# Loading weight blocks from two hardware queues in the first stage of a cross-attention kernel

## The chip, the cores and the metric

The kernel runs on one core of one Trainium2 chip. Its time is device microseconds from start to end of one execution; several executions are made and their median is given. A profile is one further execution, recorded by the hardware profiler, with a time of its own. Inside it, times are counted in microseconds (us) from the start of its span. The engines are TensorE (PE in the profile; its weight loads are PEld), VectorE (DVE), ScalarE (ACT), GpSimd (POOL) and SyncE (SP). SP does no arithmetic: it issues loads and stores. ScalarE computes, and it can issue loads from a queue of its own too. A load moves data from the chip's main memory (HBM) to the on-chip memory of 128 partitions.

## The reference

The kernel computes multi-head cross-attention with a residual and a layer norm. `x` is 16 batches of 256 rows of 256 numbers; the context `c` is 16 batches of 77 rows of 192. There are 8 heads of width 256.

```python
Q = (x @ Wq).reshape(16, 256, 8, 256).transpose(0, 2, 1, 3)
K = (c @ Wk).reshape(16, 77, 8, 256).transpose(0, 2, 1, 3)
V = (c @ Wv).reshape(16, 77, 8, 256).transpose(0, 2, 1, 3)
score = einsum('bhqd,bhkd->bhqk', Q, K) / sqrt(256)
score = where(mask, score, -inf)
attn = softmax(score, axis=-1)
out = einsum('bhqk,bhkd->bqhd', attn, V).reshape(16, 256, 2048) @ Wo + x
out = (out - mean(out)) * rsqrt(var(out) + 1e-5) * gamma + beta
```

All data is float32. Wq is 256 x 2048, Wk and Wv are 192 x 2048, Wo is 2048 x 256.

## The kernel before

**What is folded.** Per head, scores need x Wq Wk^T c^T. The kernel first forms G = Wk Wq^T per head (tiles `gA` for the first 128 context features, `gB` for the other 64), then a = G^T c^T per batch and head (`pa` in PSUM, `a` in the on-chip memory), and then scores = x a. In the same way it forms Wv Wo per head (`pu`, `pw`; `uA`, `uB`). So there is a first stage of some 53 us that works on weights, and then a loop over 16 batches which works on x.

**The first stage.** Heads are taken in four pairs, a = 0 to 3. For pair 0, Wk and Wq are loaded as natural rows (`wk_nat`, two loads of `wq_nat`, two of `wk_last`), and TensorE transposes them: `turn_k` (L666), `turn_q(0)` and `turn_q(1)` (L658) and `turn_k_last` (L672). ScalarE and VectorE copy the results from PSUM: L667 (ScalarE, kT), and for each `turn_q` one copy on VectorE and one on ScalarE (both L661). `g_of(e)` multiplies the two (L753) and ScalarE scales the result into `gA` (L756). `turn_c` turns the first context rows, loaded as `c_sb` (L690; copies L121 and L123). `rest_of_g` makes `gB` (L763, L770). `a_of_pairs` makes `a` for the first four batches (L173 and L185 on TensorE, copies L811 on ScalarE).

For pairs 1 to 3, Wk and Wq are loaded as blocks: the 128 partitions are taken as four groups of 32, and each group is one load of one pair's Wk (96 KB, tile `wk_blk`) or Wq (128 KB, tile `wq_blk`), in rows of 512 bytes. `load_blocks` issues the four loads of one pair and matrix (L576). VectorE transposes the 32 x 32 blocks (`turn_blk`, L679, two instructions a pair: Wk, then Wq), and `g_of_pair` (L777, scaled by ScalarE at L785) and `rest_of_g_of_pair` (L793, scaled by VectorE at L802) follow.

**The order of work.** It is written out by hand: each engine executes its instructions in the order of the program, and only waits for data or buffers. At the end of the stage's front part the calls are

```python
turn_k()
turn_q(0)
g_of(0)
turn_q(1)
turn_k_last()
g_of(1)
turn_c()
rest_of_g()
turn_blk(1)
a_of_pairs(0)
for a in range(1, NF):
    g_of_pair(a)
    if a == 2:
        turn_blk(3)
    rest_of_g_of_pair(a)
```

with `turn_blk(2)` and `a_of_pairs(1)` at the end of the round a = 1. All loads stand ahead of this, on SP's queue, in this order: `wk_nat`, two of `wq_nat`, two of `wk_last`, `c_sb`, then for each pair 1 to 3 four of `wk_blk` and four of `wq_blk`, then 16 of `wvT`, four of `wo` (the last two go into the place of `wq_blk` and wait until that has been read), six for the rest of the context (`load_rest`), the mask (`bias`) and two sets of transposed x (`load_xT`). ScalarE issues no load; its first instruction is the load of its function table (L609). TensorE starts with 12 transposes of an identity matrix, whose result is not used (`keep_busy`, L640).

Each load tells of its landing on one of eight semaphores, which are given to the loads in turn.

Of the kernel before, what the change touches and what calls it, by code (L numbers as in the profile page):

```python
# [17 lines left out]
D = 256  # L18
EPS = 1e-05
GB = 4  # L20
# [5 lines left out]
def kernel(  # L26
# [13 lines left out]
    nc = tc.nc  # L40
    B, S, DI = x.shape
# [6 lines left out]
    GT = GB * QT  # L48
    NF = H // 2
    KR = S2 - KM  # L50
    BK = 32
    NM = P // BK
# [53 lines left out]
    def flat(ap):  # L106
        return ap.rearrange("p a b -> p (a b)")

    def half(i):
        return slice(i * LB, (i + 1) * LB)  # L110
# [7 lines left out]
    def evacuate(dst, src):  # L118
        evacs[0] += 1
        if evacs[0] % 2:  # L120
            nc.scalar.copy(dst, src)  # L121
        else:
            nc.vector.tensor_copy(dst, src)  # L123
# [5 lines left out]
    def in_two(name, shape, g):  # L129
        return pools[g % 2].tile(shape, F32, tag=f"{name}{g % 2}", name=f"{name}_{g}", bufs=1)  # L130

    def load_xT(g, lo=0, hi=GT):


        if lo == 0:
            xT_of[g] = in_two("xT", [P, GT * NM, 2, BK], g)
        rows = x.rearrange("b s d -> (b s) d")[(g * GT + lo) * P : (g * GT + hi) * P, :]
        rows = rows.rearrange("(m r) (i n) -> i r m n", r=BK, i=NM)
        for i in range(NM):
            nc.sync.dma_start(  # L140
                xT_of[g][i * BK : (i + 1) * BK, lo * NM : hi * NM].rearrange(
                    "p m n q -> p m (n q)"
                ),
                rows[i],
            )
# [412 lines left out]
    with tc.tile_pool(name="wonce", bufs=1) as wp:  # L558
# [4 lines left out]
        wq_nat = wp.tile([P, 2, 2 * D], F32, tag="wq", name="wq_nat")  # L563
# [3 lines left out]
        wq_blk = wp.tile([P, NF - 1, DI // BK, P], F32, tag="wqb", name="wq_blk")  # L567
        wk_blk = wp.tile([P, NF - 1, NL, P], F32, tag="wkb", name="wk_blk")
        wq_blocks = wq.rearrange("(m r) (a i f) -> a i r m f", r=BK, a=NF, i=NM)
        wk_blocks = wk.rearrange("(m r) (a i f) -> a i r m f", r=BK, a=NF, i=NM)  # L570
        wq_rows = wq[:, : 2 * D].rearrange("(t p) f -> p t f", p=P)
        wk_ends = wk[P:, : 2 * D].rearrange("r (e f) -> r e f", e=2)

        def load_blocks(to, blocks):
            for i in range(NM):
                nc.sync.dma_start(to[i * BK : (i + 1) * BK], blocks[i])  # L576


        rest = slice(first * CR, None)
# [2 lines left out]
        def load_rest():  # L582

            blocks = c.rearrange("b k l -> (b k) l")[rest].rearrange("(m r) l -> r m l", r=BK)
            for l in range(NL):
                i, of = (l, cA) if l < NM else (l - NM + LB // BK, cB)
                nc.sync.dma_start(
                    flat(of)[i * BK : (i + 1) * BK, rest].rearrange("p (m q) -> p m q", q=BK),
                    blocks[:, :, l * BK : (l + 1) * BK],
                )  # L590
# [7 lines left out]

        nc.sync.dma_start(wk_nat, wk[:P, : 2 * D])
        for e in range(2):  # L600
            nc.sync.dma_start(wq_nat[:, :, e * D : (e + 1) * D], wq_rows[:, :, e * D : (e + 1) * D])
        for e in range(2):
            nc.sync.dma_start(wk_last[half(e)], wk_ends[:, e])
        nc.sync.dma_start(c_sb, c_rows[:, :first, :])
        for a in range(1, NF):
            load_blocks(wk_blk[:, a - 1], wk_blocks[a])
            load_blocks(wq_blk[:, a - 1], wq_blocks[a])

        nc.scalar.preload_act_table_set("natural_log_exp_and_others")  # L609

        wvT = wp.tile([P, NF, NL, P], F32, tag="wvT", name="wvT")
        wo_of = [
            wp.tile([P, 2, 4, DI], F32, tag=tag, name=f"wo_{i}") for i, tag in enumerate(("wo", "wqb"))
        ]
        wv_blocks = wv.rearrange("(m r) (a i f) -> a i r m f", r=BK, a=NF, i=NM)
        wo_rows = wo.rearrange("(a p n) f -> a p n f", p=P, n=4)
        for a in range(NF):
            load_blocks(wvT[:, a], wv_blocks[a])
        for a in range(NF):
            nc.sync.dma_start(wo_of[a // 2][:, a % 2], wo_rows[a])  # L620
        load_rest()
        mask_row = mask.rearrange("b k -> (b k)")

        def load_bias(lo, hi):
            nc.sync.dma_start(
                bias_f[:, lo * S2 : hi * S2].bitcast(I32),
                mask_row[lo * S2 : hi * S2].partition_broadcast(P),
            )

        load_bias(0, GB)  # L630
        load_xT(0, 0, GT // 2)
        load_xT(0, GT // 2, GT)
        load_bias(GB, B)


        idle = ps_mm.tile([P, P], F32, tag="mm", name="idle")

# [16 lines left out]
        def turn_q(e):  # L654
            for dc, copy in enumerate((nc.vector.tensor_copy, nc.scalar.copy)):
                pt = ps_mm.tile([P, 2, P], F32, tag="mm", name=f"pt_q_{e}_{dc}")
                for t in range(2):
                    nc.tensor.transpose(  # L658
                        pt[:, t], wq_nat[:, t, e * D + dc * P : e * D + (dc + 1) * P], ident
                    )  # L660
                copy(qT[:, e, dc], flat(pt))  # L661

        def turn_k():
            pt = ps_mm.tile([P, 4, P], F32, tag="mm", name="pt_k")
            for n in range(4):
                nc.tensor.transpose(pt[:, n], wk_nat[:, n * P : (n + 1) * P], ident)  # L666
            nc.scalar.copy(kT_03[:, 0, :, :P], pt)  # L667
# [9 lines left out]
        def turn_blk(a):  # L677
            for blk, of in ((wk_blk, kT_blk), (wq_blk, qT_blk)):
                nc.vector.transpose(  # L679
                    of[a].rearrange("p n (m r) -> p m n r", r=BK),  # L680
                    blk[:, a - 1].rearrange("p m (n c) -> p m n c", c=BK),
                )

        def turn_c():
            for r in range(0, first, 2):
                n = min(2, first - r)
                pc = ps_mm.tile([P, 4, P], F32, tag="mm", name=f"pc_{r}")
                for lc in range(2):
                    for j in range(n):
                        nc.tensor.transpose(  # L690
                            pc[:, 2 * lc + j, :CR],
                            c_sb[:, r + j, lc * LB : lc * LB + P],
                            ident[:CR, :CR],
                        )
                rows = slice(r * CR, (r + n) * CR)
                evacuate(flat(cA)[:, rows].rearrange("p (j m) -> p j m", m=CR), pc[:, :n, :CR])
                evacuate(
                    flat(cB)[LB:, rows].rearrange("p (j m) -> p j m", m=CR),
                    pc[LB:, 2 : 2 + n, :CR],
                )  # L700
                nc.gpsimd.tensor_copy(flat(cB)[:LB, rows], flat(cB)[LB:, rows])
# [47 lines left out]
        def g_of(e):  # L749

            pg = ps_mm.tile([P, DI], F32, tag="mm", name=f"pg_{e}")
            for dc in range(2):
                nc.tensor.matmul(  # L753
                    pg, kT[:, e, dc, :P], qT[:, e, dc], start=(dc == 0), stop=(dc == 1)
                )
            nc.scalar.mul(gA[:, e], pg, D ** -0.5)  # L756

        def rest_of_g():

            ph = ps_mm.tile([P, DI], F32, tag="mm", name="ph")  # L760
            for dc in range(2):
                for e in range(2):
                    nc.tensor.matmul(  # L763
                        ph[half(e)],
                        kT[:, e, dc, P:],
                        qT[:, e, dc],
                        start=(dc == 0),
                        stop=(dc == 1),
                    )
            nc.vector.tensor_scalar(gB[:, 0], ph, D ** -0.5, None, ALU.mult)  # L770

        def g_of_pair(a):

            banks = [ps_mm.tile([P, DI], F32, tag="mm", name=f"pgb_{a}_{e}") for e in range(2)]
            for n in range(4):
                for e in range(2):
                    nc.tensor.matmul(  # L777
                        banks[e],
                        kT_blk[a][half(e), n, :P],
                        qT_blk[a][half(e), n],  # L780
                        start=(n == 0),
                        stop=(n == 3),
                    )
            for e, o in enumerate(banks):
                nc.scalar.mul(gA[:, 2 * a + e], o, D ** -0.5)  # L785
# [26 lines left out]

        turn_k()
        turn_q(0)
        g_of(0)
        turn_q(1)
        turn_k_last()
        g_of(1)
        turn_c()
        rest_of_g()  # L820
        turn_blk(1)
        a_of_pairs(0)
        for a in range(1, NF):
            g_of_pair(a)
            if a == 2:
                turn_blk(3)
            rest_of_g_of_pair(a)
            if a == 1:
                turn_blk(2)
                a_of_pairs(1)  # L830
# [190 lines left out]
```

## Time and profile before

| | |
|---|---|
| Median of 3 runs | 274.46 us (274.32 to 274.80) |
| The profiled execution's own time | 274.61 us |
| Its span (first to last instruction) | 272.8 us |
| Around the span | 1.8 us |
| TensorE busy, share of the span | 265.8 us, 97% |
| VectorE | 214.1 us, 78% |
| GpSimd | 170.4 us, 62% |
| ScalarE | 136.2 us, 50% |
| Loads and stores | all on one hardware queue, 21.77 MB |
| Loads of `wk_blk` | 12 of 96 KB, median 4.6 us from issue to landing |
| Loads of `wq_blk` | 12 of 128 KB, median 4.7 us |
| Loads of `wvT` | 16 of 96 KB, median 3.6 us |

A line of the timeline gives start and duration in us, the engine, the line of the kernel, the operation, output <- input with their shapes, the number of instructions merged, and in brackets how long the engine had been idle before and what ended that. A line of the chain that ended last gives start, duration and what. A line of the waits gives who waited for whom, the total in us, how many times, and the longest. A line of a table by stretches gives the stretch, its length, the busy time of PE, PEld, DVE, ACT and POOL (with numbers of instructions), the TensorE clock granted, the share of time that the 16 DMA engines were busy, and GB/s. PE's busy time is modelled: the matmuls are pipelined, so that a group's duration can reach past the start of the next.

### The profile page before, as it was taken

Reading aid. Unit: us, or ns where it says so; the run is one execution under the profiler, and the core shown is the slowest. Engines: PE = TensorE matmul, PEld = TensorE weight load, DVE = VectorE, ACT = ScalarE, POOL = GpSimd, SP = SyncE. Lnnn points to the kernel's source line nnn. Section 1 sums busy time; section 2 is a strip of 40 time slices with the busy share of each in tenths; the row PEclk is TensorE's granted clock in tenths of the full one; section 3 lists DMA queues with packets and bytes.
Section 4 is the critical chain, followed back from the end, with each engine's and each line's share of the span. In section 5 each row is a group of like instructions: output and inputs, shape, how many; then the busy total and the mean of one; then the engine's idle time right before and its main releaser. Section 6 shows DMA issues by size and latency. Waiting matters only on the chain.

```text
span 272.8 us, 14124 instructions
## 1 busy us (share of the span) xinstructions
PE 265.8 (97%) x6312; PEld 194.3 (71%) x6312; DVE 214.1 (78%) x418; ACT 136.2 (50%) x444; POOL 170.4 (62%) x231
## 2 busy tenths in 40 slices
PE   7999999999999999999999999999999999999992
PEld 6557486867494949495959586867796969694662
DVE  0554938589759898979799897878798989889875
ACT  3233225363918182827364646464546372927652
POOL 1000002809887878687878777777788789845754
PEclk9999999999999999999999999999999999999999
DMA  6999989940000322310221405000504061010102
GB/s 191 194 198 189 305 160 183 278 53 2 2 5 4 88 35 73 124 44 4 70 52 36 87 19 180 31 16 9 116 2 120 2 197 41 5 43 4 61 22 77
DMA packets 42460, 22.66 MB, mean 83 GB/s; under 512 B 23632, under 2 KB 41632, under 8 KB 42400
## 3 DMA queue, kind: packets, MB, share of 16 engines
q1 hardware_dynamic: 42400, 21.77, 34.8%
q8 instruction: 49, 0.80, 1.3%
q14 instruction: 11, 0.09, 0.1%
HBM read 17.57 MB, written 4.19 MB: 80 GB/s over the span
## 4 chain that ended last, share of the span: by engine, by line
PE 89%; DMA 7%; DVE 1%; SPq 1%; issue 0%; DVEq 0%
PE ps L283 25%; PE pa L173 11%; PE po L416 10%; PE pv L208 10%; PE pm L416 9%; PE pv L219 6%; PE pa L185 5%; DMA wq_blk<-in_L_xattn_Wq_dram 5%; PE po L348 4%; PE pu L717 3%; PE pr L242 2%; DMA c_sb<-in_ctx_dram 2%; PE pw L731 1%; PE pr L254 1%; PE po L364 1%; PE pgb L777 1%
## 5 line engine op out<-in xcount | busy, mean ns | idle before, releaser
L312 ACT ACTIVATE e<-s,top 128x77 f32<-128x77 f32 x256 | 66.8, 346 | 73.4 <-DVE top L305 73.4
L283 PE MATMUL ps<-a,xT 128*32 128x154 f32 x2048 | 70.0, 294 | 0.0
L326 POOL TENSOR_TENSOR p<-e,rden 128x512 f32<-128x512 f32 x64 | 47.8, 768 | 31.8 <-DVE rden L320 16.6
L283 PEld LDWEIGHTS ps<-a,xT 128*32 128x32 f32 x2048 | 66.0, 110 | 1.5 <-issue 0.8
L298 DVE TENSOR_TENSOR s<-ps,bias 128x308 f32<-128x308 f32 x64 | 29.7, 473 | 14.7 <-PE ps L283 14.6
L449 POOL TENSOR_TENSOR xg<-xg,m 128x256 f32<-128x256 f32 x39 | 28.6, 733 | 12.8 <-DVE xg L463 10.7
L173 PE MATMUL pa<-cA,gA 128*32 128x308 f32 (+1 forms) x576 | 36.4, 394 | 0.0
L173 PEld LDWEIGHTS pa<-cA,gA 128*32 128x32 f32 x576 | 18.4, 110 | 20.3 <-issue 9.1
L208 PE MATMUL pv<-uA,cA 128*32 128x512 f32 x256 | 30.4, 592 | 0.0
L318 DVE TENSOR_REDUCE den<-e 128x8 f32<-128x616 f32 x32 | 24.9, 777 | 5.1 <-ACT e L312 4.9
L305 DVE TENSOR_REDUCE top<-s 128x8 f32<-128x616 f32 x32 | 25.4, 795 | 1.1
L336 DVE STREAM_TRANSPOSE pT<-p 128x640 f32<-128x640 f32 x32 | 25.1, 813 | 0.9 <-POOL p L326 0.9
L379 POOL TENSOR_TENSOR ts<-vw 128x768 f32<-128x768 f32 x13 | 23.9, 1839 | 0.0
L532 DVE SCALAR_TENSOR_TENSOR xg<-xg,rstd,bet 128x256 f32<-128x256 f32 x26 | 20.9, 803 | 1.9
L185 PE MATMUL pa<-cB,gB 64*32 64x308 f32 (+1 forms) x576 | 20.3, 392 | 0.0
L922 ACT COPY vw<-pv 128x512 f32<-128x512 f32 x32 | 17.1, 584 | 6.3 <-PE pv L219 6.3
L185 PEld LDWEIGHTS pa<-cB,gB 64*32 64x32 f32 x576 | 10.7, 107 | 12.3 <-issue 9.2
L594 POOL COPY cRA<-cA 128x208 f32<-128x208 f32 x1 | 0.4, 358 | 29.8 <-DVE cA L593 29.8
L416 PE MATMUL po<-vr,pT 128*32 128x128 f32 x416 | 18.5, 273 | 0.0
L922 ACT COPY a<-pa 128x308 f32<-128x308 f32 (+1 forms) x56 | 17.5, 416 | 0.0
L219 PE MATMUL pv<-uB,cB 64*32 64x512 f32 x256 | 17.4, 601 | 0.0
L463 DVE TENSOR_TENSOR xg<-po,xg 128x256 f32<-128x256 f32 x31 | 11.7, 415 | 5.0 <-PE po L416 4.6
(117 smaller groups left out, 408.7 us busy)
## 6 DMA issues: line engine op xcount, KB each, us to landing
xT<-in_x_dram SPq DMA_DIRECT2D x32, 128.0 KB, 4.4
xg<-in_x_dram SPq DMA_DIRECT2D x4, 1024.0 KB, 6.7
out_dram<-xg SPq DMA_DIRECT2D x11, 256.0 KB, 2.8
wo<-in_L_xattn_Wo_dram SPq DMA_DIRECT2D x4, 512.0 KB, 6.2
wq_blk<-in_L_xattn_Wq_dram SPq DMA_DIRECT2D x12, 128.0 KB, 4.7
wvT<-in_L_xattn_Wv_dram SPq DMA_DIRECT2D x16, 96.0 KB, 3.6
out_dram<-xg SPq DMA_DIRECT2D x10, 128.0 KB, 1.7
wk_blk<-in_L_xattn_Wk_dram SPq DMA_DIRECT2D x12, 96.0 KB, 4.6
```

Of the source, the lines that this page charges most:

```text
L173: nc.tensor.matmul(flat(o[i * BK : (i + 1) * BK]), gA[:, h, cols(dc, i)], flat(cA[:, batches, :]), start=True, stop=False,)
L185: nc.tensor.matmul(flat(banks[j + k][i * BK : (i + 1) * BK]), gB[half(k), h // 2, cols(dc, i)], flat(cB[half(k), batches, :]), start=False ...
L208: nc.tensor.matmul(pv[k][i * BK : (i + 1) * BK], cA[:, b, k * BK : (k + 1) * BK], uA[:, parts, :, i], start=True, stop=False,)
L219: nc.tensor.matmul(pv[k][i * BK : (i + 1) * BK], cB[half(k), b, k * BK : (k + 1) * BK], uB[half(k), parts, :, i], start=False, stop=True,)
L283: nc.tensor.matmul(ps[m // 2][i * BK : (i + 1) * BK, m % 2 * 2 * S2 : (m % 2 + 1) * 2 * S2], xT_of[g][:, j * NM + m, dc], flat(a_of[g][:, ...
L298: nc.vector.tensor_tensor(s[:, a * H // 2 : (a + 1) * H // 2], ps[a][:, : H // 2 * S2].rearrange("p (h k) -> p h k", k=S2), bias[:, b, :]. ...
L305: nc.vector.tensor_reduce(top, s, AX.X, ALU.max, negate=True)
L312: nc.scalar.activation(e[:, h], s[:, h], AF.Exp, bias=top[:, h : h + 1])
L326: nc.gpsimd.tensor_tensor(part, e_mh[:, :, :, keys], rden_mh.unsqueeze(3).to_broadcast(list(part.shape)), ALU.mult,)
L416: nc.tensor.matmul(out[i * BK : (i + 1) * BK], weight[:, i], moving, start=(n == 0), stop=(n == len(terms) - 1),)
L449: nc.gpsimd.tensor_tensor(to, to, what, ALU.add)
L922: nc.scalar.copy(dst, src)
```

## The change

The blocks of Wk and Wq of pairs 1 to 3 are shared between two queues: groups 0 and 2 are issued by SP, groups 1 and 3 by ScalarE. The two loads of `wq_nat` go to ScalarE's queue as well, ahead of its table load. `wk_nat`, `wk_last` and `c_sb` stay on SP.

The calls that issue the blocks are spread over the program. Ahead of the work stand pair 1's Wk (all four groups) and the SP half of its Wq. After `turn_q(0)` come ScalarE's half of pair 1's Wq and SP's half of pair 2; after `turn_c`, ScalarE's half of pair 2 and SP's half of pair 3; after `g_of_pair(1)`, ScalarE's half of pair 3, and then all later loads (`load_later`: `wvT`, `wo`, the rest of the context, the mask, x), which stay on SP in their order. On SP's queue, which only issues, the order of the loads is thus as before, without those that ScalarE has taken. What is computed is not changed.

```diff
-        def load_blocks(to, blocks):
-            for i in range(NM):
-                nc.sync.dma_start(to[i * BK : (i + 1) * BK], blocks[i])
+        def load_blocks(to, blocks, groups=range(NM), queue=nc.sync):
+            for i in groups:
+                queue.dma_start(to[i * BK : (i + 1) * BK], blocks[i])
+
+        def load_k(a, *where):
+            load_blocks(wk_blk[:, a - 1], wk_blocks[a], *where)
+
+        def load_q(a, *where):
+            load_blocks(wq_blk[:, a - 1], wq_blocks[a], *where)
+
+        by_sp, by_act = ((0, 2), nc.sync), ((1, 3), nc.scalar)
...
         nc.sync.dma_start(wk_nat, wk[:P, : 2 * D])
         for e in range(2):
-            nc.sync.dma_start(wq_nat[:, :, e * D : (e + 1) * D], wq_rows[:, :, e * D : (e + 1) * D])
+            nc.scalar.dma_start(
+                wq_nat[:, :, e * D : (e + 1) * D], wq_rows[:, :, e * D : (e + 1) * D]
+            )
+        nc.scalar.preload_act_table_set("natural_log_exp_and_others")
         for e in range(2):
             nc.sync.dma_start(wk_last[half(e)], wk_ends[:, e])
         nc.sync.dma_start(c_sb, c_rows[:, :first, :])
-        for a in range(1, NF):
-            load_blocks(wk_blk[:, a - 1], wk_blocks[a])
-            load_blocks(wq_blk[:, a - 1], wq_blocks[a])
-
-        nc.scalar.preload_act_table_set("natural_log_exp_and_others")
+        load_k(1, *by_sp)
+        load_k(1, *by_act)
+        load_q(1, *by_sp)
...
-        for a in range(NF):
-            load_blocks(wvT[:, a], wv_blocks[a])
-        for a in range(NF):
-            nc.sync.dma_start(wo_of[a // 2][:, a % 2], wo_rows[a])
-        load_rest()
...
-        load_bias(0, GB)
-        load_xT(0, 0, GT // 2)
-        load_xT(0, GT // 2, GT)
-        load_bias(GB, B)
+        def load_later():
+            for a in range(NF):
+                load_blocks(wvT[:, a], wv_blocks[a])
+            for a in range(NF):
+                nc.sync.dma_start(wo_of[a // 2][:, a % 2], wo_rows[a])
+            load_rest()
+            load_bias(0, GB)
+            load_xT(0, 0, GT // 2)
+            load_xT(0, GT // 2, GT)
+            load_bias(GB, B)
...
         turn_k()
         turn_q(0)
+        load_q(1, *by_act)
+        load_k(2, *by_sp)
+        load_q(2, *by_sp)
         g_of(0)
         turn_q(1)
         turn_k_last()
         g_of(1)
         turn_c()
+        load_k(2, *by_act)
+        load_q(2, *by_act)
+        load_k(3, *by_sp)
+        load_q(3, *by_sp)
         rest_of_g()
         turn_blk(1)
         a_of_pairs(0)
         for a in range(1, NF):
             g_of_pair(a)
+            if a == 1:
+                load_k(3, *by_act)
+                load_q(3, *by_act)
+                load_later()
             if a == 2:
                 turn_blk(3)
             rest_of_g_of_pair(a)
```

## The prediction

> **What bounds the kernel now.** I read the page first: the span and the engines' shares.
>
> ```profile
> span 272.8 us, 14124 instructions
> PE 265.8 (97%) x6312; PEld 194.3 (71%) x6312; DVE 214.1 (78%) x418; ACT 136.2 (50%) x444; POOL 170.4 (62%) x231
> ```
>
> TensorE is the bound, so a faster load is worth only the TensorE idle time that it removes. Next, the chain that ended last, from its start:
>
> ```profile
> 3.36 4.70 DMA c_sb<-in_ctx_dram
> 8.08 4.48 DMA wq_blk<-in_L_xattn_Wq_dram
> 12.58 5.48 DMA wq_blk<-in_L_xattn_Wq_dram
> 18.07 4.58 DMA wq_blk<-in_L_xattn_Wq_dram
> 22.77 1.26 DVE qT L679
> 24.17 2.00 PE pgb L777 x16
> 26.16 1.03 PE phb L793 x32
> 27.20 4.28 PE pa L173 x64
> ```
>
> Up to 22.65 us the chain is loads, each issued as an earlier one lands; from 24.17 on it is TensorE back to back. So the change can help only by moving 24.17. The waits of SP's queue say why loads are chained:
>
> ```profile
> SPq L576 <- DMA wq_blk<-in_L_xattn_Wq_dram: 2.9, 9, 0.5
> SPq L576 <- DMA c_sb<-in_ctx_dram: 0.7, 1, 0.7
> ```
>
> The chain steps from c_sb (6th load of the program) to the 14th, the 22nd and the 30th: a load waits until the one eight before it has landed, since eight completion semaphores go round. I assume that both queues share these eight, in program order. How fast the loads run, by stretches:
>
> ```profile
> 8.00:18.00 10.00, 9.96 (x146) 6.13 (x150) 4.32 (x9) 3.07 (x10) 0.59 (x2) 1.00 1.22 200
> 30.00:34.00 4.00, 4.00 (x92) 1.97 (x86) 4.00 (x4) 1.75 (x6) 0.00 (x0) 1.00 1.00 366
> ```
>
> The last number is GB/s: 200 with blocks of 32 partitions, 366 with Wo, whose tiles have 128. Last, ScalarE's timeline, for the room that its new issues find:
>
> ```profile
> 5.20 0.59 ACT L667 COPY kT<-pt_k 128x512 f32<-128x512 f32 x1 [3.19 <-PE pt_k L666]
> 6.06 0.37 ACT L661 COPY qT<-pt_q 128x256 f32<-128x256 f32 x1 [0.27 <-PE pt_q L658]
> 7.34 0.39 ACT L756 ACTIVATE gA<-pg 128x256 f32<-128x256 f32 x1 [0.91 <-PE pg L753]
> 7.78 0.37 ACT L661 COPY qT<-pt_q 128x256 f32<-128x256 f32 x1
> 9.21 0.38 ACT L756 ACTIVATE gA<-pg 128x256 f32<-128x256 f32 x1 [1.06 <-PE pg L753]
> 9.59 0.50 ACT L121 COPY cA<-pc 128x224 f32<-128x224 f32 x2
> 13.74 1.37 ACT L811 COPY a<-pa 128x308 f32<-128x308 f32 x4 [3.65 <-PE pa L185]
> 16.13 0.66 ACT L785 ACTIVATE gA<-pgb 128x256 f32<-128x256 f32 x2 [1.01 <-PE pgb L777]
> 20.11 1.38 ACT L811 COPY a<-pa 128x308 f32<-128x308 f32 x4 [3.33 <-PE pa L185]
> ```
>
> Gaps of 3.65 and 3.33 us are wide; those of 0.27 and 0.91 us are not.
>
> **What the Trainium skill says.** DMA: Bandwidth & Descriptors, "Issuing engines are not separate DMA queues": loads from SP and ScalarE run on the same 16 DMA engines and interleave; a second issuer saves only issue time. The trace agrees that issue is not the limit from 8 to 18 us: SP issues there took 0.31 to 0.45 us (one 1.45), and most still had to wait. "Anatomy of one DMA" on the same page: a semaphore wait is taken on the issuing sequencer, before dispatch. So on ScalarE whatever follows a waiting load waits too; the trace shows this for SP alone. "Queues, rings and completion order": each DMA engine goes round the queues that have work. No run here shows it, as all loads are on q1. SBUF — State Buffer, "Door 1: The DMA port swizzle (why `[64,N]` ≈ `[32,N]`)": partitions 0 to 63 use one half of the 16 ports, 64 to 127 the other; eight ports carry at most some 218 GB/s. The trace's 200 GB/s fits. Groups 0 and 1 lie in one half, 2 and 3 in the other, so two queues that each alternate the halves can be faster.
>
> **The change, part by part.**
>
> Removed at the end of the stage: the last wait for Wq. The 32 matmuls of L793 that began at 22.55 end about 23.59, as the next such group took from 26.09 to 27.13. L777 began at 24.17: 0.58 us of stall. Its cause is the landing at 22.65; the transpose of that block could otherwise start at 21.43, when the one of Wk before it ends, and end at 22.68. In the first pair the same wait costs about 0.08: the matmuls of L185 from 12.90 take 1.12 (64 of them took 2.24 from 31.41 to 33.65), so they end at 14.02, and L777 began at 14.10. Most that can be won: 0.66 us.
>
> Will the last blocks come in time? ScalarE reaches the four loads of pair 3 after the scaling of L785, which ends at 16.79. Four issues at 0.45 put the last at 18.14, begun as early as before (18.07). By then SP has sent its own blocks, and only four of Wv can stand beside them: the fifth needs the semaphore of a ScalarE block. With a latency between 3.1 (Wv's shortest) and 4.6 us it lands between 21.2 and 22.8; I take 21.6. The transpose then runs to about 22.9, before 23.59. If it lands later than 22.3, the stall returns one for one. (Whatever delays the front moves all of these alike.) These issues take 1.8 of a gap of 3.33 us, so the copies of L811 are not delayed. Those of pair 2, 1.8 us after the copies that end at 10.09, wait for blocks of pair 1 (landed at 12.56 at the latest before) and end about 13.0, ahead of 13.74: nothing, with 0.7 us in hand.
>
> Moved at the front: the two loads of Wq's natural rows leave SP (0.93 us of issue). SP reaches c_sb some 0.98 us sooner, at 2.4. On ScalarE they are issued from 0.73 on, and the table load of 1.28 us ends near 3.0, long before 5.20: hidden. But Wk's rows, which TensorE awaits at 4.05, now share the DMA engines with Wq's. If Wk's 256 KB come first the cost is 0; if Wq's 256 KB come first it is 256 KB at the 320 GB/s of 4 to 5 us, 0.8 us. I take 0.3. All of TensorE's work up to 24.17 follows in order, with little slack. It can't gain: nothing can land before the first load.
>
> Added on ScalarE: ten issues in all, two waits of which are dear. The second Wk block of pair 1 takes the semaphore of the first Wq load (issued at 1.17, landed 3.7 us later, at 4.84, before), so ScalarE is free at about 5.3 instead of for the copy of 5.20. That copy then ends near 5.9, and TensorE's L753 needed it at 6.20: nothing, unless Wq lands late.
>
> The second Wq block of pair 1 takes the semaphore of c_sb, which landed at 8.06. Behind it on ScalarE stand the scaling of L756 (7.34) and the copy of L661 (7.78), and TensorE's second half of L753 waits for that copy. With c_sb landed at t, ScalarE is free at t + 0.02 + 0.40; scaling and copy, with a little dead time, end 0.84 later. TensorE needs the copy at about 8.50, halfway through the 1.13 us of the L753 group from 8.04. So the delay is t + 1.26 - 8.50 = t - 7.24. With t as before it is 0.82. c_sb is issued earlier, but the bytes to be moved by its end are the same 1.1 MB, and a Wk block from ScalarE may mix in (96 KB, 0.3 us). Against this there are idle moments in the DMA engines before (5 to 6 us: share 0.77), and the 32-partition blocks behind c_sb now fall on both port halves. I take t = 7.75: delay 0.5, bounds 0 (t = 7.2) and 1.2 (t = 8.45). It contains the delay of the front, as the c_sb wait doesn't move with TensorE: the larger counts, not their sum. I take 0.55 for both.
>
> Moved back: Wv, Wo, the rest of c, bias and x follow in the same order on SP. The fifth Wv load went at 20.58 and goes when Wk's ScalarE block has landed, near 20.4; three more wait for ScalarE's other blocks, to 21.6, and the last eight follow at 0.48 each, to 25.4 (26.75 before). Wv's transposes began at 28.50 straight after other VectorE work, so this costs nothing; its cover is about 1 us for Wo (landed at 32.62, needed at 33.65). A second queue might add to the 1.8 us around the span; no row prices it; I take 0, bounds -0.1 and +0.3.
>
> Sum: -0.58 - 0.08 + 0.55 = -0.1 us. Against the profiled execution's own time of 274.61 that gives 274.5; the median of the runs is 0.15 lower at 274.46, so 274.4.
>
> **The rivals.** *ScalarE isn't held up.* c_sb lands by 7.2 and Wk's rows are not late. For it: the earlier issue, both port halves, the DMA engines' idle shares. Against it: the same bytes ahead. Worth -0.55 to -0.66: 273.85.
>
> *ScalarE's wait for c_sb becomes the bound.* It decides from a landing of 8.45 on, when the delay of 1.2 is more than 0.66 + 0.55. Place: L661 behind the load, L753 behind that. For it: 8.06 already, with 96 KB more to mix in. Against it: the earlier issue. At t = 8.8 the delay is 1.56, less 0.66: 275.4.
>
> *The last blocks are no sooner.* ScalarE's issues of pair 3 stretch, as one of SP's took 1.45 us, so that the stall stays and the 0.55 of the front is added: 275.0, just on the slower side.
>
> **How the numbers follow.** One can tell about 0.2% (0.55 us) from no change here. Near-balance 0.40, with a range of its own from 273.95 to 274.95; not held 0.28; bound by c_sb 0.24; last blocks late 0.08. Faster 0.28, same 0.40, slower 0.32. The range 273.75 to 275.4 leaves out the far ends of the rivals, some 0.2.
>
> **What would show it.** Right: L777 of pair 3 follows L793 with no wait on the transpose, 0.1 us or so from 24.17; the load of Wq's group 3 of pair 1 on ScalarE's queue begins as c_sb lands; the copy of L661 stands after it near 9.0, and TensorE idles up to 0.5 us before L753's second half. Wk's first transposes begin at 4.05 to 4.5. Wrong: loads that do not wait for the eighth before them on the other queue, a TensorE gap elsewhere before 27 us, or a wait on Wv or Wo after it.

## The result, and the profile after

The change makes the kernel slower: 278.44 us (277.94 to 278.53, 4 runs) against 274.63 us (274.32 to 275.48, 4 runs). The ratio is 1.013, with a 95% interval from 1.0104 to 1.0156. The forecast of 274.4 us missed, and 278.44 lies outside its range of 273.75 to 275.4 too. The profiled executions differ by as much as the medians: 278.36 against 274.61 us, with spans of 276.6 and 272.8 us.

Three parts of the page after the change: the span, the engines' busy time, and the queues (packets, MB, share of 16 engines).

```profile
span 276.6 us, 14117 instructions
PE 268.0 (97%) x6312; PEld 195.5 (71%) x6312; DVE 214.1 (77%) x418; ACT 136.1 (49%) x444; POOL 170.3 (62%) x231
q1 hardware_dynamic: 38976, 19.87, 30.0%
q10 hardware_dynamic: 3424, 1.90, 3.3%
```

A second queue, q10, is in use and has 1.90 MB. So the change does what it says. The chain that ended last, after the change:

```profile
3.02 6.74 DMA wk_blk<-in_L_xattn_Wk_dram
9.79 4.40 DMA wq_blk<-in_L_xattn_Wq_dram
14.20 4.39 DMA wq_blk<-in_L_xattn_Wq_dram
18.61 3.73 DMA wvT<-in_L_xattn_Wv_dram
22.36 4.05 DMA wq_blk<-in_L_xattn_Wq_dram
26.50 1.25 DVE qT L688
27.89 2.00 PE pgb L786 x16
29.89 1.03 PE phb L802 x32
30.92 4.28 PE pa L173 x64
```

Before, four loads followed one another (c_sb and three blocks of Wq) and the last Wq block landed at 22.65 us. Now there is one link more, and it is a block of **Wv**, which the kernel needs much later. The last Wq block waits for the slot of that Wv block, is issued at 22.36 and lands at 26.41, 3.76 us later than before. `pgb` of pair 3 (L786, before L777) moves from 24.17 to 27.89. The loss is all there by then: L283, the scores of the first batch, moves from 53.27 to 57.00, which is 3.73 again.

TensorE is late well before that. Three lines of its timeline before the change:

```profile
6.20 1.10 PE L753 MATMUL pg<-qT,kT 128*128 128x256 f32 x4 [0.18 <-DVE qT L661]
10.69 2.28 PE L173 MATMUL pa<-cA,gA 128*32 128x308 f32 x32
22.55 1.10 PE L793 MATMUL phb<-qT,kT 64*64 64x128 f32 x32
```

And after the change, from the first transposes to the stall (L762 and L802 were L753 and L793):

```profile
4.64 1.11 PE L675 MATMUL pt_k<-ident,wk_nat 128*128 128x128 f32 x4 [0.45 <-DMA wk_nat<-in_L_xattn_Wk_dram]
7.03 2.05 PE L762 MATMUL pg<-qT,kT 128*128 128x256 f32 x4 [0.18 <-DVE qT L670]
10.15 0.92 PE L762 MATMUL pg<-qT,kT 128*128 128x256 f32 x2
11.31 0.70 PE L762 MATMUL pg<-qT,kT 128*128 128x256 f32 x2 [0.24 <-ACT qT L670]
13.53 2.28 PE L173 MATMUL pa<-cA,gA 128*32 128x308 f32 x32
25.39 1.10 PE L802 MATMUL phb<-qT,kT 64*64 64x128 f32 x32
27.89 2.00 PE L786 MATMUL pgb<-qT,kT 64*128 64x256 f32 x16 [1.40 <-DVE qT L688]
```

L173 of pair 0 begins at 13.53 instead of 10.69, so the front (the work ahead of L173) has lost 2.84 us. Three things show: Wk's rows come 0.6 us later; the first group of L762 takes 2.05 us for what took 1.10; and its last part waits for a copy on ScalarE. From there to L802 nothing more is lost (25.39 against 22.55 is 2.84 again). Without the stall of 1.40 us, L786 of pair 3 would have begun near 26.4. Two bounds therefore end at the same place: the front alone would put it near 26.4, the loads put it at 27.89.

ScalarE's timeline after the change (its load issues are the lines marked ACTq):

```profile
4.62 0.33 ACTq L576 DMA_DIRECT2D wk_blk<-in_L_xattn_Wk_dram  x1
7.91 2.66 ACTq L576 DMA_DIRECT2D wq_blk<-in_L_xattn_Wq_dram  x2
10.61 0.38 ACT L765 ACTIVATE gA<-pg 128x256 f32<-128x256 f32 x1 [3.35 <-PE pt_kl L681]
10.89 0.37 ACT L670 COPY qT<-pt_q 128x256 f32<-128x256 f32 x1
18.97 0.66 ACT L794 ACTIVATE gA<-pgb 128x256 f32<-128x256 f32 x2 [0.87 <-PE pgb L786]
19.80 0.81 ACTq L576 DMA_DIRECT2D wk_blk<-in_L_xattn_Wk_dram  x2
21.43 1.25 ACTq L576 DMA_DIRECT2D wq_blk<-in_L_xattn_Wq_dram  x2
```

The two Wq loads of pair 1 keep ScalarE from its last copy (ended at 7.25) to 10.57. The first waits until ScalarE's own first Wk block has landed (7.88), the second until its other one has (10.23). So the scaling and the copy behind them (7.34 and 7.78 before) come at 10.61 and 10.89. The four loads of pair 3 come only from 19.80 on. SP does not stand still meanwhile. Its timeline from 13 us to the issue of the last Wq block:

```profile
14.78 7.46 SPq L576 DMA_DIRECT2D wvT<-in_L_xattn_Wv_dram  x9
```

Nine blocks of Wv, 96 KB each, went ahead of the last Wq block; before, none did. At the rate of these loads that is 9 x 98,304 bytes / 200 GB/s = 4.4 us, of the size of the 3.76 us lost. A slot here is one of the eight semaphores, which a load can use when the load that used it last has landed. Two lines of the waits of SP's queue show that both queues share the eight slots, as SP waits for loads that ScalarE issued (`wq_nat`):

```profile
SPq L576 <- DMA wq_nat<-in_L_xattn_Wq_dram: 3.3, 2, 2.2
SPq L576 <- DMA c_sb<-in_ctx_dram: 1.0, 1, 1.0
```

The second line shows that c_sb's slot went to a load of SP, not to ScalarE's Wq block as I had assumed. Last, the rate (the last number, GB/s) after the change:

```profile
8.00:18.00 10.00, 9.76 (x101) 6.01 (x101) 3.87 (x7) 2.81 (x9) 0.59 (x2) 1.00 1.09 202
18.00:26.00 8.00, 7.92 (x145) 4.86 (x145) 4.23 (x7) 2.64 (x9) 0.00 (x0) 1.00 0.94 190
```

Two queues move 202 GB/s from 8 to 18 us where one moved 200. This agrees with the Trainium skill, DMA: Bandwidth & Descriptors, "Issuing engines are not separate DMA queues": all loads run on the same 16 engines. The second queue changes the order of the loads and does not raise their rate.

### The profile page after: what moved, and what is told of

The parts are those of the page before. It is cut to its first block, busy times and chain, and to the rows that moved or that the text cites. A ratio compares the mean times of both kernels' runs of the same rounds, so it can differ in the third digit from the quotient of the medians.

```text
span 276.6 us, 14117 instructions
## 1 busy us (share of the span) xinstructions
PE 268.0 (97%) x6312; PEld 195.5 (71%) x6312; DVE 214.1 (77%) x418; ACT 136.1 (49%) x444; POOL 170.3 (62%) x231
## 4 chain that ended last, share of the span: by engine, by line
PE 88%; DMA 8%; DVE 1%; SPq 1%; issue 0%; DVEq 0%
PE ps L283 24%; PE pa L173 11%; PE po L416 10%; PE pv L208 10%; PE pm L416 9%; PE pv L219 6%; PE pa L185 5%; DMA wq_blk<-in_L_xattn_Wq_dram 5%; PE po L348 4%; PE pu L726 3%; DMA wk_blk<-in_L_xattn_Wk_dram 2%; PE pr L242 2%; DMA wvT<-in_L_xattn_Wv_dram 1%; PE pw L740 1%; PE pr L254 1%; PE po L364 1%
## 5 line engine op out<-in xcount | busy, mean ns | idle before, releaser
L283 PE MATMUL ps<-a,xT 128*32 128x154 f32 x2048 | 70.0, 294 | 0.0
L283 PEld LDWEIGHTS ps<-a,xT 128*32 128x32 f32 x2048 | 66.0, 110 | 1.5 <-issue 0.8
L173 PE MATMUL pa<-cA,gA 128*32 128x308 f32 (+1 forms) x576 | 36.4, 394 | 0.0
L173 PEld LDWEIGHTS pa<-cA,gA 128*32 128x32 f32 x576 | 18.4, 110 | 20.3 <-issue 9.1
L185 PE MATMUL pa<-cB,gB 64*32 64x308 f32 (+1 forms) x576 | 20.3, 392 | 0.0
L185 PEld LDWEIGHTS pa<-cB,gB 64*32 64x32 f32 x576 | 10.7, 106 | 12.3 <-issue 9.2
```

The source lines that it names most:

```text
L173: nc.tensor.matmul(flat(o[i * BK : (i + 1) * BK]), gA[:, h, cols(dc, i)], flat(cA[:, batches, :]), start=True, stop=False,)
L185: nc.tensor.matmul(flat(banks[j + k][i * BK : (i + 1) * BK]), gB[half(k), h // 2, cols(dc, i)], flat(cB[half(k), batches, :]), start=False ...
L283: nc.tensor.matmul(ps[m // 2][i * BK : (i + 1) * BK, m % 2 * 2 * S2 : (m % 2 + 1) * 2 * S2], xT_of[g][:, j * NM + m, dc], flat(a_of[g][:, ...
```

## The experiments

The first four took the late front to be the cause. Theory A has two causes side by side there (ScalarE held, matmuls at half pace), B takes ScalarE's hold for the whole loss, C the half pace, and D says that loads from two queues are slower as such.

**q1_on_sp.** Kernel after, with ScalarE's two Wq loads of pair 1 issued by SP, so that nothing holds the copy of L670.

```diff
-        load_q(1, *by_act)
+        load_q(1, (1, 3), nc.sync)
```

> The changed kernel, but the two blocks of pair 1's Wq (groups 1 and 3) are issued by SP at the same place of the program, so that ScalarE is not held up ahead of the scaling and the copy. Theory A (two causes side by side: ScalarE is held until 10.57 us, and TensorE's matmuls run at half pace until about 10.6 us, so that either alone would keep the second half of pg of head 1 back): only some 0.5 us come back, 277.9 us; that half begins near 10.8 instead of 11.31, and the transposes pt_q still last 421 ns. Theory B (the hold of ScalarE is the whole of the 2.0 us between the first transposes and pa): 276.4 us, and that half begins near 9.4.

Measured: 276.75 us median, ratio 1.0094 [1.0061, 1.0127]. TensorE's timeline:

```profile
8.72 1.13 PE L762 MATMUL pg<-qT,kT 128*128 128x256 f32 x4
23.23 1.10 PE L802 MATMUL phb<-qT,kT 64*64 64x128 f32 x32
26.49 3.37 PE L786 MATMUL pgb<-qT,kT 64*128 64x256 f32 x16 [2.16 <-DVE qT L688]
```

The hold is gone and the front has won back 2.16 us (L802 at 23.23 instead of 25.39), but L786 of pair 3 waits that long instead, for a last Wq block that landed at 24.98. So the front is not the bound here. The median and the place of L762's last part are near what B expected, but not for B's reason: the first group of L762 took 1.10 us in this profile too, so that the 2.16 us belong to the hold and the slow pace together, and what bounds is the load. The matmuls after the stall are slow (3.37 us for 2.00, and 1.36 for 1.10), some 1.6 us of the 1.8 by which the profiled execution (278.57 us, the longest of the six) is above the median.

**busy** and **q1_on_sp_busy.** Six more of the transposes whose result isn't used, to keep TensorE working between the first loads; in the second kernel with the edit of q1_on_sp as well.

```diff
-        keep_busy(12)
+        keep_busy(15)
...
         turn_k()
+        keep_busy(1)
         turn_q(0)
+        keep_busy(2)
```

> The changed kernel with six more unused transposes on TensorE: 15 instead of 12 at the start, one after turn_k, two after turn_q(0), to fill the gaps that late loads leave, so that TensorE looks busy without a break. Theory A: the matmuls go to full pace early (the second pt_q transposes of 272 ns instead of 421), but ScalarE is still held until 10.57, so the time stays within 0.3 us of 278.4. Theory C (the slow matmuls are the whole of the 2.0 us): 276.5 us. Theory B: no change in the matmuls' durations, 278.4.

> Both of the edits: pair 1's Wq wholly from SP, and six more unused transposes. Theory A: now neither cause is left, and about 2.0 us come back: 276.4 us, with pa of pair 0 beginning near 11.5 instead of 13.53. Theories B and C: no better than the one of the two single edits that each names (B: as with Wq from SP alone; C: as with the transposes alone).

Measured: 281.52 us, 1.0254 [1.0216, 1.0292], and 279.17 us, 1.0156 [1.0121, 1.0191]: both slower than without the transposes, which no theory expected. From the timelines of TensorE and SP (up to the last Wq block's issue) in busy:

```profile
6.92 1.10 PE L762 MATMUL pg<-qT,kT 128*128 128x256 f32 x4
10.86 0.70 PE L762 MATMUL pg<-qT,kT 128*128 128x256 f32 x2 [1.41 <-ACT qT L670]
29.27 2.51 PE L786 MATMUL pgb<-qT,kT 64*128 64x256 f32 x16 [3.19 <-DVE qT L688]
14.97 8.14 SPq L576 DMA_DIRECT2D wvT<-in_L_xattn_Wv_dram  x10
```

The matmuls reach full pace in time, and L762 still waits for ScalarE's copy until 10.86: the hold alone makes the front 2.39 us late (L173 of pair 0 at 13.08 instead of 10.69), and in the kernel after the half pace alone kept TensorE busy until 11.07, just short of the copy. So they act in parallel. But the last block came at 27.75, with ten Wv blocks ahead of it. L283 begins at 59.94, 2.94 us later than in the kernel after: L786 of pair 3 begins 1.38 later, and it and L802 behind it take 0.51 and 0.88 us longer. Why the loads came later with more transposes was not found. A, B and C fall as causes of the total.

**wq_q1_on_sp.** Wq's natural rows go back to SP too.

```diff
-            nc.scalar.dma_start(
+            nc.sync.dma_start(
                 wq_nat[:, :, e * D : (e + 1) * D], wq_rows[:, :, e * D : (e + 1) * D]
...
-        load_q(1, *by_act)
+        load_q(1, (1, 3), nc.sync)
```

> The changed kernel with the two loads of Wq's natural rows back on SP, and pair 1's Wq wholly from SP. Theory A: Wk's rows land near 4.0 again instead of 4.59, TensorE is busy early, the matmuls go to full pace near 6.3 us as before, and pa of pair 0 begins near 10.7: 2.84 us come back, 275.6 us; what stays is the longer wait for the last blocks of pair 3, about 1 us. Theory D (two queues slow the loads as such, whoever issues them first): Wk's rows still land past 4.3, and the time is 276.5 or more.

Measured: 276.42 us, 1.0066 [1.0044, 1.0088]. L802 of pair 2 begins at 23.50, the last block lands at 24.91, L786 starts at 26.38 after a wait of 1.78 us. A missed, and D's marks came: Wk's rows landed at 4.43 and not near 4.0, `pa` of pair 0 begins at 11.65, and the time is D's but for 0.1 us. The rows still share the DMA engines, now with two Wk blocks that ScalarE issues at 0.76 and 1.18. So this run leaves D standing.

From these runs comes theory **E**: Wv overtakes the blocks of pair 3, since SP's stream isn't tied to the program position of ScalarE's loads. Four more runs were made on E, on D, and on **P** (loads in alternating port halves are faster, whatever the queue).

**p3_on_sp.** Kernel after, with only pair 3's groups 1 and 3 moved to SP, ahead of Wv. The late front stays.

```diff
-                load_k(3, *by_act)
-                load_q(3, *by_act)
+                load_k(3, (1, 3), nc.sync)
+                load_q(3, (1, 3), nc.sync)
                 load_later()
```

> The changed kernel, but groups 1 and 3 of pair 3's Wk and Wq are issued by SP, at the same place of the program, so that on SP's queue they stand ahead of Wv. Theory E (Wv overtakes them: while ScalarE's issues for pair 3 wait, SP sends nine Wv blocks, 885 KB, ahead of the last block): the last block lands by 25.0 us instead of 26.41, pgb of pair 3 follows phb of pair 2 at 26.4 with no wait for VectorE, and the 1.46 us of that wait come back: 276.9 us. Theory D (two queues are slower as such): the last block lands at 26 us or later, and the time stays at 278 us.

Measured: 277.21 us, 1.0099 [1.0066, 1.0132]; the profiled execution took 276.63. TensorE's timeline:

```profile
10.93 0.70 PE L762 MATMUL pg<-qT,kT 128*128 128x256 f32 x2 [0.36 <-ACT qT L670]
25.01 1.10 PE L802 MATMUL phb<-qT,kT 64*64 64x128 f32 x32
26.04 2.00 PE L786 MATMUL pgb<-qT,kT 64*128 64x256 f32 x16
```

The last block landed at 22.44, 4 us earlier than in the kernel after, though ten loads still go by ScalarE's queue, and L786 follows L802 with no wait. D, which had it at 26 us or later, falls as the cause of the late block. What is left is the late front, 26.04 - 24.17 = 1.9 us over before. So the loads and the front are two bounds, each of about 2 us alone (L786 at 26.38 in wq_q1_on_sp, 26.04 here), as E says.

**wq_q1_p3_on_sp.** All three moves together. ScalarE keeps six loads: groups 1 and 3 of pair 1's Wk and of pair 2.

```diff
-            nc.scalar.dma_start(
+            nc.sync.dma_start(
                 wq_nat[:, :, e * D : (e + 1) * D], wq_rows[:, :, e * D : (e + 1) * D]
...
-        load_q(1, *by_act)
+        load_q(1, (1, 3), nc.sync)
...
-                load_k(3, *by_act)
-                load_q(3, *by_act)
+                load_k(3, (1, 3), nc.sync)
+                load_q(3, (1, 3), nc.sync)
```

> The changed kernel with three of its moves undone: Wq's natural rows, pair 1's Wq and pair 3 are issued by SP; on ScalarE's queue stay groups 1 and 3 of pair 1's Wk and of pair 2. Theory E: nothing overtakes, the last block lands near 23 us, pgb of pair 3 begins near 24.5 (TensorE's front is still 0.9 us late, as pair 1's Wk on ScalarE is sent ahead of Wq's rows): 275.0 us. Theory D: as with Wq and pair 1 on SP alone, 276.4 us.

Measured: 276.43 us, 1.0052 [1.0027, 1.0077], from 274.73 to 277.77 over 12 runs. The profiled execution is one of the short ones, 274.92 us: last block at 22.08, L786 at 24.47 with no wait, L283 at 53.58. This execution is what E expected, and three of the twelve are of its length (274.73 to 274.92). The other nine took 276.15 us or more, and the median is D's 276.4, not E's 275.0. The profile of a short run can't say why, so for the time of this kernel E is not shown.

**b_0213.** Kernel before, one queue, with the groups of every block in the order 0, 2, 1, 3.

```diff
-            for i in range(NM):
+            for i in (0, 2, 1, 3):
```

> The kernel before, with the four groups of every block load issued in the order 0, 2, 1, 3, so that on its one queue neighbouring loads fall on different halves of the partitions. Theory P (the 200 GB/s of these loads are a limit of the half of the ports that a group uses): the rate between 8 and 18 us rises over 215 GB/s, the last block of pair 3 lands before 22.0 instead of 22.65, and the time falls by up to 0.58 us. Theory N (the limit is the same for any order): 200 GB/s, 274.4 us, no difference.

Measured: 274.19 us against 274.90, ratio 0.9968 [0.9953, 0.9984]: **faster than before by 0.3%**, the only kernel here that is. From the table by stretches:

```profile
8.00:18.00 10.00, 9.92 (x145) 5.99 (x146) 4.21 (x9) 3.29 (x11) 0.59 (x2) 1.00 1.16 213
```

The rate is 213 GB/s instead of 200, the last block lands at 21.30 instead of 22.65, and L777 of pair 3 begins at 23.86 with no wait. The Trainium skill, SBUF — State Buffer, "Door 1: The DMA port swizzle (why `[64,N]` ≈ `[32,N]`)", gives a possible reason: groups 0 and 1 lie in one half of the ports, 2 and 3 in the other. The runs show the effect of the order, not that the ports are its cause. The rate is clear of the 196 to 206 GB/s of the four profiles in which SP issues the groups in the order 0, 1, 2, 3 (before, b_wq_act, b_fill, b_cold), but 2 GB/s short of what P expected. That the earlier block is what made the kernel faster is not shown: this profiled execution took 274.73 us, no less than that of before, though L283 begins at 52.97 instead of 53.27, and the kernel one_queue below has the same rate and as early a block and is no faster than before.

**b_fill.** Kernel before, with `a` of pair 2 computed ahead of pair 3's `pgb`, to fill the wait.

```diff
             rest_of_g_of_pair(a)
             if a == 1:
                 turn_blk(2)
                 a_of_pairs(1)
+            if a == 2:
+                a_of_pairs(2)
...
-        a_of_pairs(2, 3)
+        a_of_pairs(3)
```

> The kernel before, with its loads as they are, but the a of pair 2 is made ahead of G of pair 3 (a_of_pairs(2) after rest_of_g_of_pair(2), then a_of_pairs(3) at the end), so that TensorE has 3.3 us of work while the last block is awaited. If the wait for the last block is the one stall there, 0.58 us come back: 273.9 us, and pgb of pair 3 starts with no wait for VectorE. If VectorE or ScalarE is late with gB or gA of pair 2, no gain or a loss of some 0.5 us.

Measured: 274.93 us, 1.0003 [0.9986, 1.0019]: no difference. L777 of pair 3 has no wait any more, but L717 begins at 33.46 instead of 33.65 and not 0.58 earlier. Done in two parts, `a` of pairs 2 and 3 takes 6.82 us of TensorE (two stretches of 3.41) where together it took 6.52, and the stage stood 0.10 behind before it: 0.58 - 0.30 - 0.10 = 0.18.

**p3_early.** Kernel after, with ScalarE's four loads of pair 3 issued right behind its loads of pair 2.

```diff
         load_k(3, *by_sp)
         load_q(3, *by_sp)
+        load_k(3, *by_act)
+        load_q(3, *by_act)
...
             if a == 1:
-                load_k(3, *by_act)
-                load_q(3, *by_act)
                 load_later()
```

> Kernel after, but ScalarE issues its four loads of pair 3 (groups 1 and 3 of Wk and Wq) right behind its loads of pair 2, before the start of Wv on SP; same blocks, same two queues. Theory E (Wv overtakes ScalarE's late loads on the shared slots): the last Wq block lands by 22.8 us instead of 26.41, so L786 of pair 3 follows L802 with no wait on the last block, bound by the late front at 26.0 to 26.5; device time 276.6 to 277, as with these blocks on SP. Theory D (a load from ScalarE's queue is served later as such): the last block still lands at 25.5 or later, 278.4. A third outcome, H: the four loads wait for slots on ScalarE and hold the copies of L820 and the scaling of L794 behind them; then the block lands early but pa or phb of pair 1 is late by up to 1.5 us, and the time is 277.5 to 278.4.

Measured: 281.54 us, 1.0237 [1.0197, 1.0278], outcome H, and larger than I had it. From the timelines of ScalarE, TensorE and SP (up to the last Wq block's issue):

```profile
19.24 2.73 ACTq L576 DMA_DIRECT2D wq_blk<-in_L_xattn_Wq_dram  x2
22.02 1.37 ACT L820 COPY a<-pa 128x308 f32<-128x308 f32 x4 [9.26 <-DMA wq_blk<-in_L_xattn_Wq_dram]
23.73 3.93 PE L173 MATMUL pa<-cA,gA 128*32 128x308 f32 x32 [3.93 <-ACT gA L794]
14.76 6.82 SPq L576 DMA_DIRECT2D wvT<-in_L_xattn_Wv_dram  x7
```

Issued early, the loads wait in front of the copies of L820, and TensorE stands still for 3.93 us. And they aren't early: the last of them takes the slot of ScalarE's own last block of pair 2, which lands at 21.64, and by then seven Wv blocks have passed. E's landing by 22.8 did not come (25.75), and the run does not tell E from D by the landing. That D has little for it is seen in the trace of the kernel after: ScalarE's loads of pair 3 took 3.80 to 4.05 us from issue to landing, SP's smaller Wv loads issued from 19.48 to 22.86 3.67 to 3.95.

**b_wq_act** and **b_cold.** Two parts of the front on the kernel before: Wq's rows alone from ScalarE, and 1 instead of 12 unused transposes at the start.

```diff
-            nc.sync.dma_start(wq_nat[:, :, e * D : (e + 1) * D], wq_rows[:, :, e * D : (e + 1) * D])
+            nc.scalar.dma_start(wq_nat[:, :, e * D : (e + 1) * D], wq_rows[:, :, e * D : (e + 1) * D])
```

```diff
-        keep_busy(12)
+        keep_busy(1)
```

> Kernel before, with Wq's two natural-row loads alone issued from ScalarE. It is the front part of the change without any load that ScalarE has to wait for. Theory E with a front term: Wk's rows land 0.4 to 0.6 us later (4.01 before), so the first transposes begin at 4.4 to 4.6; ScalarE is not held, so L773-like work follows; pair 3 stays bound by its last block, which lands at 22.4 to 22.9; device time 274.5 to 275.1. Rival W (the later start also shifts the moment when TensorE's matmuls reach full pace): L753's first group takes 2 us instead of 1.1, pa of pair 0 begins at 11.8 or later instead of 10.69, and the time is 275.6 to 276.2.

> Kernel before with 1 instead of 12 of the unused transposes of L640 at the start (nothing of the result is left out). It asks what decides when TensorE's matmuls go from half to full pace and what that moment is worth. Theory W: it needs work ahead of it, so without the transposes the doubling moves from about 6.2 us to 8 us or later, pg's groups take 2 us, pa of pair 0 begins at 11.8 to 12.6 (10.69 before), L777 of pair 3 is bound by TensorE at about 25.3 to 26, and the time is 275.7 to 276.4. Rival (the moment does not depend on those transposes): pace as before, pa at 10.7, 274.5.

Measured: b_wq_act 274.79 us, 1.0004 [0.9977, 1.0031]. Wk's transposes begin at 4.43 instead of 4.05, L777 of pair 3 at 24.04: sharing the first loads costs nothing in the end, because pair 3's block comes no later. b_cold 275.43 us, 1.0022 [1.0012, 1.0033]. Its first L753 group on TensorE's timeline, and L777 of pair 3:

```profile
6.14 1.81 PE L753 MATMUL pg<-qT,kT 128*128 128x256 f32 x4 [0.18 <-DVE qT L661]
24.23 2.00 PE L777 MATMUL pgb<-qT,kT 64*128 64x256 f32 x16
```

Full pace comes during that group or just after it, and pa of pair 0 starts at 11.33 instead of 10.69. In this profile the 0.64 us is nearly all taken up by the wait before L777. The median loses 0.2%, more than the rival and less than W expected; the profiled execution (274.65 us) is the shortest of the 20 and doesn't show where.

**one_queue.** Kernel after in its own written order, but groups 1 and 3 on SP too. Only Wq's natural rows stay on ScalarE.

```diff
-        by_sp, by_act = ((0, 2), nc.sync), ((1, 3), nc.scalar)
+        by_sp, by_act = ((0, 2), nc.sync), ((1, 3), nc.sync)
```

> Kernel after with groups 1 and 3 of every block on SP's queue too: the written order of after (groups 0 and 2 of a block, then 1 and 3, Wv behind pair 3) stays, and of ScalarE's loads only Wq's two natural rows. Theory E (the loss lies in the second queue: Wv overtakes, and ScalarE is held): Wk's rows still share (first transposes at 4.4 to 4.6 us), but the scaling of L765 and the copy of L670 are free by 8.3, the last Wq block lands at 21.3 to 22.7, L786 of pair 3 begins at 23.9 to 24.4, device time 274.2 to 274.9. Rival O (the new written order of the loads costs, whatever the queue): the last block still lands at 24 or later, 276 to 278.

Measured: 274.57 us, 1.0003 [0.9988, 1.0018]. L786 of pair 3 begins at 23.76 with no wait. From the table by stretches:

```profile
8.00:18.00 10.00, 9.92 (x144) 6.01 (x146) 4.31 (x9) 3.25 (x10) 0.59 (x2) 1.00 1.15 213
```

One word undoes the whole loss. The written order costs nothing (rival O falls); it is the second queue for the blocks. The groups come in the order 0, 2, 1, 3 here too, and the loads again run at 213 GB/s. The eight kernels that give blocks to ScalarE's queue have 198 to 205 GB/s there, with each queue's groups in alternating halves too: so what the order gains on one queue, 4 to 7%, is not seen with two. That much of D stands; how it comes about was not tested.

The kernels by the profiled execution, without b_fill, whose order of work differs. Counted are the Wv blocks that SP issued before the last Wq block:

| Kernel | Wv blocks ahead | Last Wq block lands | L786 (L777) of pair 3 | Its wait |
|---|---|---|---|---|
| b_0213 | 0 | 21.30 | 23.86 | none |
| one_queue | 0 | 21.68 | 23.76 | none |
| b_cold | 0 | 21.89 | 24.23 | none |
| wq_q1_p3_on_sp | 0 | 22.08 | 24.47 | none |
| p3_on_sp | 0 | 22.44 | 26.04 | none |
| b_wq_act | 0 | 22.52 | 24.04 | 0.18 |
| before | 0 | 22.65 | 24.17 | 0.51 |
| wq_q1_on_sp | 4 | 24.91 | 26.38 | 1.78 |
| q1_on_sp | 5 | 24.98 | 26.49 | 2.16 |
| p3_early | 7 | 25.75 | 31.75 | none (held before) |
| q1_on_sp_busy | 6 | 25.77 | 27.36 | 3.30 |
| after | 9 | 26.41 | 27.89 | 1.40 |
| busy | 10 | 27.75 | 29.27 | 3.19 |

Over the landing of before it is some 0.4 to 0.6 us a block (2.26 us for four, 5.10 for ten), and 98,304 bytes at 200 GB/s take 0.49. Where the wait is above 0.5 us, L786 starts 1.5 to 1.6 us after the landing, the transpose of 1.25 us and a little dead time.

## Why the prediction was wrong

**The last blocks.** The step that failed is "only four of Wv can stand beside them" with its landing at 21.6, and the bracket behind it, "Whatever delays the front moves all of these alike". It does not. ScalarE's loads of pair 3 stand behind the scaling of L794 of pair 1 and move with the front (that scaling ended at 16.79 before, at 19.63 now). SP's stream moves with nothing but landings. So each us by which the front is late lets some two more Wv blocks pass: nine instead of four. By L802 of pair 2 the front is 0.95 and 0.68 us late in wq_q1_on_sp and q1_on_sp, with four and five Wv blocks, and 2.84 and 2.43 us late in the kernel after and in busy, with nine and ten. Nor were the four priced: where the four passed, the block landed at 24.91, which is 2.3 us after the 22.65 of before; 4 x 98,304 bytes / 200 GB/s are 2.0. I had checked that the issues came in time and left out the bytes ahead of them. Also the four issues took not 0.45 us each but waited for slots: the last was to come at 18.14, and came at 22.36, when a Wv block had landed. In wq_q1_on_sp it came at 20.12, when a Wq block of SP had landed (20.10). So a block taken to land at 21.6 landed at 26.41.

**ScalarE held.** The mechanism was right: a waiting load holds the copy behind it. This is what the Trainium skill, DMA: Bandwidth & Descriptors, "Anatomy of one DMA", let one expect, and the trace of the kernel after now shows it on ScalarE (until 10.57). The load and the size were wrong. The slots do not go round in program order, as I had assumed for both queues; the second Wq load of pair 1 began as ScalarE's own Wk block of group 3 landed (10.23), and c_sb's slot went to SP. With t = 10.23 my own formula, t - 7.24, gives 3.0 us; the copy came at 10.89 instead of 7.78, 3.1 later. I had used t = 7.75 and 0.5.

**The front's first loads.** The shift of Wk's rows was 0.58 us (4.01 to 4.59) where I took 0.3, within my bounds of 0 to 0.8. It counts for little, as b_wq_act shows.

**The wait in the first pair.** The 0.08 us there was no wait for a load. L777 began 1.20 us after L185 before, and L786 does so after (15.74 to 16.94), where the transpose had ended at 16.09. So of the 0.66 us only 0.58 was a stall.

**Sum.** In place of -0.58 - 0.08 + 0.55 stand +3.7 by the loads and, hidden under it, +2.2 by the front (26.4 - 24.17). The two do not add, but they are not apart either: the front's delay made the loads later. Undoing most of the front alone (wq_q1_on_sp) leaves 276.42 us, undoing the loads alone (p3_on_sp) 277.21.

**Rivals.** "c_sb becomes the bound" and "last blocks are no sooner" were the right side, each too small, and I had let neither feed the other. That no wait on Wv or Wo comes later held. That pair 2's loads cost nothing on ScalarE held too, but without the 0.7 us in hand: they ended at 16.68, and the copies of L820 behind them began at 16.72, 0.98 us after L185 instead of 0.84; nothing waited for them. That two queues which each alternate the halves can be faster did not come true (202 GB/s).

**Open.** Why wq_q1_p3_on_sp, with six loads left on ScalarE, has a median 1.5 us above its profiled execution isn't settled; nor is how much of its time, and of the others', the lower rate of two queues costs. How far the moment of TensorE's full pace makes the spread of the runs isn't either. And b_0213 was 0.3% faster while one_queue was not.

## What to carry to other kernels

Ahead of splitting a stream of loads over two queues, ask what the first queue will send when the second is held up: loads of lower urgency can pass, and each costs about its bytes over the shared rate (here 0.4 to 0.6 us for 96 KB). On an engine that computes, a load can wait for a slot, and everything behind it waits too, as here on ScalarE. The order of the targets on one queue is worth a try: here 0, 2, 1, 3 raised the rate from 200 to 213 GB/s, which two queues did not, though a faster kernel came of it in only one case of two.

## What the runs showed of the hardware

TensorE's matmuls have two paces, which the column of the granted clock (1.00 from 8 to 18 us in the tables by stretches) does not show. In groups of TensorE's instructions by shape, from 4 to 13 us, before and after:

```profile
L753 PE MATMUL pg<-qT,kT 128*128 128x256 f32 x8 | 2.2, 401 | 0.3 <-DVE qT L661 0.2
```

```profile
L762 PE MATMUL pg<-qT,kT 128*128 128x256 f32 x8 | 3.7, 582 | 0.4 <-ACT qT L670 0.2 <-DVE qT L670 0.2
```

The mean is 401 ns before and 582 after, since full pace came near 6 us in one profile and after 10 in the other; in the other kernels' profiles it came between some 4.3 (b_fill) and 10 us (p3_on_sp). The Trainium skill, TensorE: Matmul & The Clock Gate, "Part 1: The HAM clock gate (the "warmup" mystery)", says that the array runs at half clock until a window of some 3.4 us has been busy, and that the moment varies from run to run. That it varies fits; how long TensorE must be busy is not shown here. It also says that an idle window of that length brings the half clock back; here the matmuls were slow already after waits of 2.16 us (q1_on_sp: 3.37 us for 2.00) and 3.3 us (q1_on_sp_busy: 2.76 for 2.00), and after 3.93 (p3_early: 3.93 for 2.28), though not after 1.78 (wq_q1_on_sp: 2.00). So a stall of TensorE can cost more than its own length.
